# A two-layer transformer block: attention with undivided probabilities, and values by seven half-size products

## The chip, the cores and the metric

The kernel runs on one core of a Trainium2 chip. A core has a matrix engine (TensorE, PE in the profile, with its weight loads as PEld), a vector engine (VectorE, DVE), an engine for activation functions (ScalarE, ACT), a general one (GpSimd, POOL) and a queue that issues DMA transfers (SyncE, SP). Each engine works through its own instructions in the order in which they were written; semaphores hold an instruction back until what it needs is there. TensorE writes to eight banks of PSUM (2 KB in each of 128 partitions); everything else lies in SBUF or in DRAM. The metric is the time of one execution on the device in microseconds, the median of several runs.

## What is computed

The input x has 8 batches of 512 tokens with 256 channels, all in float32. The first layer adds to x a causal attention with 16 heads of 64 channels on the normalised input, and an int8 matrix product of that input. The second layer adds a gated comparison and a recurrent-style feed-forward part. Cut to the attention, which is what matters here:

```python
def _L0_attn_ref(x, Wq, bq, Wk, bk, Wv, bv, Wo, bo):
    q = (x @ Wq + bq).reshape(b, s, H, L)
    k = (x @ Wk + bk).reshape(b, s, H, L)
    v = (x @ Wv + bv).reshape(b, s, H, L)
    q = _apply_rope(q, cos, sin)
    k = _apply_rope(k, cos, sin)
    ...
    scores = jnp.einsum('bnqd,bnkd->bnqk', q, k) / jnp.sqrt(jnp.float32(L))
    scores = jnp.where(causal, scores, -1000000000.0)
    attn = jax.nn.softmax(scores, axis=-1)
    attended = jnp.einsum('bnqk,bnkd->bnqd', attn, v)
    attended = jnp.transpose(attended, (0, 2, 1, 3)).reshape(b, s, H * L)
    return attended @ Wo + bo

x = x + _L0_attn_ref(xn, ...) + _L0_ffn_ref(xn, ...)
xn = _layernorm(x, axis=-1)
x = x + _L1_attn_ref(xn, ...) + _L1_ffn_ref(xn, ...)
```

## The kernel before

The attention is worked through in 16 groups, `at` = 0 to 15: a batch `b` = at // 2 and a half `g` = at % 2 of its heads, so 8 heads a group. Everything is written in one fixed order by hand, and each engine keeps to it; there is no scheduler.

For each group the stages are these (line numbers are those of the profile of before):

- **project** (`project_qk`, matmuls at L428): queries and keys, four matmuls of 512 columns each for two half-groups. A float32 matmul appears as two instructions in the profile. ScalarE moves each bank out with its bias (L434, `l`), four DMAs on SP make a copy with neighbouring partition blocks exchanged (`y`, L436), VectorE multiplies `l` and `y` by the cosine and sine tables (L446, 128x1024 each; called rotations below), and GpSimd adds the two (L461). The tiles `l` and `y` exist twice.
- **project_v** (L472): the values of a group, for 512 tokens and 512 columns, as four banks of two matmuls (the 256 channels are contracted in two halves of 128). ScalarE copies each bank out (L478), and SP stores the result in DRAM (`va`); `load_v` loads it back in another layout (`vr`).
- **scores** (L509): 16 query blocks of 32, in five runs, 0 to 4: run 0 holds the blocks 15, 14 and 0, run 1 holds 13, 1, 12 and 2, and so on to run 4, which holds block 7. A block sees only the keys up to its own place.
- **soften**: VectorE adds the causal mask, writes the masked scores into a tile `p` and finds their maxima (L537); ScalarE takes the exponential and its sums (L541).
- **divide**: VectorE inverts the sums of a run (L552), and GpSimd multiplies each block's probabilities by them (L560; ScalarE in two places, L558).
- **turn** (L580): VectorE transposes a run's probabilities in 32x32 blocks into the tiles `t`.
- **weigh** (L597): TensorE multiplies the values by the transposed probabilities, into four banks; it needs all five runs of its group. **keep_weighed** (L611): ScalarE copies the four banks out and adds the values' bias.
- **finish**: `output_product` (L390), two banks of 128x256 products with Wo, and `add_output` (L399), which adds them to x in `x1s` on VectorE.

The main loop runs over `at` = 1 to 14 and is one pass of a pipeline over several groups. In the order of writing a pass holds: scores of run 0 of `at`; turn of run 4 of `at - 1`; soften; weigh and keep_weighed of `at - 1`; rotations of the keys of `at + 1`; divide; run 1; turn of run 0; projection of the queries of `at + 1`; run 2; rotations of their first half; turn of run 1; values of `at + 1`; run 3; rotations of the second half; turn of run 2; run 4; finish of `at - 1`; turn of run 3; projection of the keys of `at + 2`; divide. Into some passes other work is set: normalising the input of a later batch (`look_at`, `prepare`, passes 2, 3, 5, 7, 9 and 11), turning it by transposes and DMAs (`turn_x`), and the int8 product of two batches (`add_quantised`, passes 12 and 13). After pass 14, which ends behind the values, the last two groups are written out by hand together with the first steps of the second layer, and then a loop runs over the 8 batches of the second layer.

PSUM banks are handed out in turn, eight in all, each free again when its last reader has finished. TensorE's matmuls, in the order of a pass: sc (run 0), av, sc (run 1), pq, sc (run 2), pv, sc (runs 3 and 4), pw, pq.

## Time and profile before

| what | value |
|---|---|
| three runs | 935.48, 935.68, 936.91 us; median 935.68 |
| span of the profiled execution | 934.3 us |
| granted TensorE clock in it | 1.000 |
| weighings of passes 1, 7, 8 and 14 start at | 72.52, 344.75, 388.99, 658.81 us |
| last weighing (group 15) starts at | 729.87 us |

One execution was recorded by the hardware profiler; its span is the time from its first to its last instruction. The page lists busy time by engine, then a chain that is followed back from the last instruction: at each step to what released it, or to the instruction before it on the same engine. A timeline row gives start, duration, engine, line, operation, `out<-in`, shapes, the number of instructions merged into the row, and in brackets the idle time before it and what ended that. Starts of consecutive instructions on one engine can lie closer than their durations, since they overlap a little.

Over a pass in the middle of the loop, from 318.2 to 362.4 us, TensorE was busy for 44.20 of 44.20 us, VectorE for 39.40, ScalarE for 26.32 and GpSimd for 27.35.

### The profile page before, as it was taken

To read this page: it belongs to the slowest core of one execution; us is meant where nothing else is said; L and a number is where in the kernel's file an instruction comes from. 1 tells how busy PE (TensorE), PEld (TensorE's weight loads), DVE (VectorE), ACT (ScalarE), POOL (GpSimd) and SP (SyncE) were. 2 spreads that over 40 slices of the span, in tenths; PEclk is the share of its full clock that TensorE was granted. 3 is DMA by queue.
4 is the path that set the end of the run, shared out by engine and by line. 5 is a ranking of instruction groups with operands and counts; after the bars stand their busy time and mean duration, and the time that the engine had idled before them with its cause. 6 is when DMAs were issued, how large, how long until landed. Compare 5 with 4: busy or idle time off the path is not lost.

```text
span 934.3 us, 27432 instructions
## 1 busy us (share of the span) xinstructions
PE 919.8 (98%) x10451; PEld 594.7 (64%) x10451; DVE 793.3 (85%) x2441; ACT 528.3 (57%) x1478; POOL 542.2 (58%) x688
## 2 busy tenths in 40 slices
PE   9998999999999999999999999999999999999998
PEld 5446565656566575757565656566657777777776
DVE  4998898898899889988998899999899588888854
ACT  3585564647465646474746556555577444445553
POOL 2576766655665667566665756678667323444311
PEclk9999999999999999999999999999999999999999
DMA  7667354525543464245444635563435133221011
GB/s 213 194 165 213 102 138 130 121 75 132 169 105 97 109 182 132 75 115 172 123 95 114 179 93 145 151 154 97 110 108 127 47 102 79 74 50 48 25 33 34
DMA packets 70290, 108.03 MB, mean 116 GB/s; under 512 B 8592, under 2 KB 49040, under 8 KB 70160
## 3 DMA queue, kind: packets, MB, share of 16 engines
q1 hardware_dynamic: 68288, 104.64, 42.2%
q10 hardware_dynamic: 1872, 1.64, 0.7%
q8 instruction: 83, 1.36, 0.6%
q14 instruction: 47, 0.39, 0.1%
HBM read 41.76 MB, written 28.84 MB: 76 GB/s over the span
## 4 chain that ended last, share of the span: by engine, by line
PE 85%; DVE 6%; DMA 3%; issue 1%; POOL 1%; SPq 1%; ACT 1%; DVEq 0%; ACTq 0%; POOLq 0%
PE pq L428 21%; PE av L597 14%; PE sc L509 11%; PE pw L390 10%; PE pv L472 8%; PE po L756 6%; PE pk L703 3%; PE pg L718 3%; PE pvv L730 3%; DVE t L580 2%; PE c L675 2%; PE trc L743 1%; PE plr L245 1%; DVE p L537 1%; DMA xnl<-xnf 1%
## 5 line engine op out<-in xcount | busy, mean ns | idle before, releaser
L541 ACT ACTIVATE p<-p,nm 128x64 f32<-128x64 f32 (+15 forms) x512 | 260.0, 512 | 123.8 <-DVE nm L537 100.9
L560 POOL TENSOR_SCALAR p<-p,rs 128x512 f32<-128x512 f32 (+4 forms) x504 | 265.4, 547 | 44.6 <-DVE rs L552 42.6
L461 POOL TENSOR_TENSOR h<-h,y 128x1024 f32<-128x1024 f32 x62 | 161.1, 2598 | 181.5 <-DVE y L446 102.2
L537 DVE CUSTOM_DVE_ANT_0 p<-sc,cmask 128x64 f32<-128x64 f32 (+15 forms) x512 | 190.2, 434 | 53.7 <-PE sc L509 53.7
L580 DVE STREAM_TRANSPOSE t<-p 128x256 f32<-128x256 f32 (+3 forms) x640 | 192.2, 367 | 17.9 <-POOL p L560 17.8
L509 PE MATMUL sc<-h,h 64*32 64x512 f32 (+15 forms) x4096 | 138.7, 393 | 1.3 <-POOL h L461 1.2
L597 PE MATMUL av<-t,vr 32*64 32x384 f32 (+15 forms) x4096 | 128.8, 392 | 3.7 <-issue 3.7
L597 PEld LDWEIGHTS av<-t,vr 32*64 32x64 f32 x4096 | 122.8, 131 | 9.2 <-issue 7.9
L509 PEld LDWEIGHTS sc<-h,h 64*32 64x32 f32 x4096 | 78.6, 106 | 78.5 <-issue 58.3
L434 ACT ACTIVATE l<-pq,cs 128x512 f32<-128x512 f32 x128 | 84.7, 683 | 67.6 <-PE pq L428 53.3
L390 PE MATMUL pw<-wo,att 128*128 128x256 f32 x512 | 114.9, 382 | 0.8 <-DVE nm L537 0.8
L446 DVE TENSOR_TENSOR y<-y,cs 128x1024 f32<-128x1024 f32 x64 | 110.6, 1728 | 5.1 <-DMA y<-l 5.1
L428 PE MATMUL pq<-xnT,wq 128*128 128x512 f32 x256 | 114.6, 599 | 0.2 <-ACT xnT L349 0.2
L428 PE MATMUL pq<-xnT,wk 128*128 128x512 f32 x256 | 113.1, 593 | 1.4 <-DVE x L399 1.0
L472 PE MATMUL pv<-wv,xnT 128*128 128x512 f32 x256 | 114.3, 599 | 0.0
L390 PEld LDWEIGHTS pw<-wo,att 128*128 128x128 f32 x512 | 95.9, 190 | 19.5 <-issue 6.1
L541 ACT ACTIVATION_READ_ACCUMULATOR p<-p,nm 128x1 f32 x512 | 97.3, 190 | 0.0
L428 PEld LDWEIGHTS pq<-xnT,wk 128*128 128x128 f32 x256 | 48.3, 190 | 58.2 <-issue 55.4
L472 PEld LDWEIGHTS pv<-wv,xnT 128*128 128x128 f32 x256 | 47.3, 190 | 57.9 <-issue 54.5
L446 DVE TENSOR_TENSOR h<-l,cs 128x1024 f32<-128x1024 f32 x64 | 80.0, 1252 | 4.3 <-ACT l L434 4.3
L428 PEld LDWEIGHTS pq<-xnT,wq 128*128 128x128 f32 x256 | 47.2, 190 | 56.0 <-issue 48.8
L611 ACT ACTIVATE att<-av,cs 128x512 f32<-128x512 f32 x64 | 38.7, 688 | 71.3 <-PE av L597 71.3
(114 smaller groups left out, 940.7 us busy)
## 6 DMA issues: line engine op xcount, KB each, us to landing
y<-l SPq DMA_DIRECT2D x256, 128.0 KB, 2.3
va<-v SPq DMA_DIRECT2D x32, 512.0 KB, 3.1
vr<-va SPq DMA_DIRECT2D x64, 256.0 KB, 5.1
x<-in_x SPq DMA_DIRECT2D x15, 512.0 KB, 5.0
x1f<-x SPq DMA_DIRECT2D x7, 512.0 KB, 3.2
out<-y SPq DMA_DIRECT2D x14, 256.0 KB, 2.2
xnf<-xs SPq DMA_DIRECT2D x5, 512.0 KB, 3.6
xnT<-xnf SPq DMA_DIRECT2D x20, 128.0 KB, 2.8
```

The lines of the kernel that those rows point to most:

```text
L390: nc.tensor.matmul(pw[:, j, :], atts[at, p][:, tok], wo[:, 4 * (at % NH) + p, :], start=(p == 0), stop=(p == 3),)
L428: nc.tensor.matmul(pb.rearrange("p (t a r) -> p t a r", a=4, r=Q), w[:, g, k, bass.ts(t, P)], xnT[b][:, k].rearrange("p a (t r) -> p t a r ...
L434: nc.scalar.activation(l[:, t, :], pb, AF.Identity, bias=cs[:, bias : bias + 1])
L446: nc.vector.tensor_tensor(dst, src, table[:, None, :].to_broadcast([P, 2, S]), ALU.mult)
L461: (engine or nc.gpsimd).tensor_tensor(h, h, y, ALU.add)
L472: nc.tensor.matmul(pb.rearrange("p (g n) -> p g n", g=2), xnT[b][:, k, 2 * half + j], wqkv[2][:, 2 * g : 2 * g + 2, k, :], start=(k == 0), ...
L509: nc.tensor.matmul(scored[at, i][e][j * Q : j * Q + Q, :], q[rows, j % 2, bass.ts(i, Q)], k[rows, j % 2, :n], start=True, stop=True,)
L537: nc.vector.tensor_tensor_reduce(p[:, e, col : col + n], sc, cmask[:, S - n :], -1.0 / L**0.5, BIG, ALU.add, ALU.min, nm[:, c : c + 1],)
L541: nc.scalar.activation(p[:, e, col : col + n], p[:, e, col : col + n], AF.Exp, bias=nm[:, c : c + 1], scale=-1.0, accum_out=sm[:, c : c + 1],)
L560: nc.gpsimd.tensor_scalar(p, p, rs[:, c : c + 1], 1.0, ALU.mult, ALU.mult)
L580: nc.vector.transpose(turned[at][c][:, :, at_ : at_ + (n - 1) * pitch(c) + 1 : pitch(c), :], p[:, :, c * P : c * P + n * Q].rearrange("p e ...
L597: nc.tensor.matmul(banks[j][e * L : e * L + L, i * Q :], vs[at][rows, c, m, bass.ts(e, L)], t[c][rows, e, m * pitch(c) + m : m * pitch(c) ...
```

## The change

The probabilities stay undivided, so `divide` and all calls of it are gone. When the last run of a group has been turned, `settle` inverts all sums of the group at once, transposes them on VectorE, writes them to DRAM and loads them back as a tile `share`, in which each head's 64 partitions hold its reciprocal sums along the tokens. `keep_weighed` multiplies the weighted values by it, on GpSimd, and for the last group half of them on VectorE. Its bias is no longer added there: `gather_bias` multiplies Wo's rows by the values' bias and adds them up, once, and `spread_bias` sums over partitions with a matmul of ones and adds the result to the output's bias.

The values of groups 2 to 15 are computed by Strassen's scheme in Winograd's form: seven products of half the size, each two matmuls of 256 columns, in place of eight. It needs sums of the weights (`sum_weights`, once, the block `a21` overwritten), differences of the input (`mix_input`, once a batch), and additions of the products. Four of the products go to one bank `x` one after the other, with a copy after each; one goes to `y`, two to `z`.

In the loop, the output product of `at - 1`, which stood behind run 4, now stands between run 2 and run 3: its first half ahead of the seven products, its second half between them as two `fillers`. In pass 14 there are no fillers.

```diff
@@ -379,19 +378,41 @@
+        def gather_bias():
+            both = line("bvwo").rearrange("p (j n) -> p j n", j=2)
+            ones = line("ones")[:, :P]
+            nc.gpsimd.memset(ones, 1.0)
+            for p in range(NP):
+                bv = BIAS + 2 * NP + p
+                nc.gpsimd.tensor_scalar(
+                    both[:, min(p, 1), :], wo[:, p, :], cs[:, bv : bv + 1], None, ALU.mult
+                )
+                if p:
+                    nc.gpsimd.tensor_tensor(both[:, 0, :], both[:, 0, :], both[:, 1, :], ALU.add)
+            nc.gpsimd.tensor_tensor(bob, bob, rw[:, 2, :], ALU.add)
+            gathered[0] = ones, both[:, 0, :]
+
+        def spread_bias():
+            pb = bank("bvwo")
+            nc.tensor.matmul(pb[:, :D], *gathered.pop(0), start=True, stop=True)
+            nc.vector.tensor_tensor(bob, pb[:, :D], bob, ALU.add)
...
-        def output_product(at, half):
+        def output_product(at, half, js=(0, 1)):
...
@@ -481,6 +502,84 @@
+        def sum_weights():
+            one, two, three = (wv_sums[:, :, n] for n in range(3))
+            (a11, a12), (a21, a22) = ([wv[:, :, h, k] for k in range(NK)] for h in range(2))
+            for dst, x, y, op in (
+                (one, a21, a22, ALU.add), (two, one, a11, ALU.subtract),
+                (a21, a11, a21, ALU.subtract), (three, a12, two, ALU.subtract),
+            ):
+                nc.gpsimd.tensor_tensor(dst, x, y, op)
...
+        def mix_input(b):
+            t = work.tile([P, 4, 2, P], F32, tag="tx", name=f"tx_{b}")
+            (b11, b12), (b21, b22) = ([xnT[b][:, k, 2 * h : 2 * h + 2] for h in range(2)] for k in range(NK))
+            for dst, x, y in ((0, b12, b11), (1, b22, t[:, 0]), (2, b22, b12), (3, b21, t[:, 1])):
+                nc.gpsimd.tensor_tensor(t[:, dst], x, y, ALU.subtract)
+            mixes[b] = t
+
+        def project_v_by_seven(at, fillers=(None, None), between=lambda: None):
...
+            def product(to, left, right, fresh=False):
+                for j in range(2):
+                    nc.tensor.matmul(
+                        to[:, j, :], left[:, j], right, start=fresh and j == 0, stop=True,
+                        skip_group_check=j > 0 or not fresh,
+                    )
...
+            def keep(half, g_):
+                nc.scalar.copy(part(half, g_), of(x))
+
+            def add(bank_, half, g_):
+                nc.vector.tensor_tensor(part(half, g_), of(bank_), part(half, g_), ALU.add)
...
+            product(x, b11, a11, True)
+            keep(0, 0)
+            product(y, b21, a12, True)
+            product(z, t1, s1, True)
+            product(x, t2, s2)
+            keep(1, 0)
+            add(y, 0, 0)
+            if fillers[0]:
+                fillers[0]()
+            product(x, t3, s3)
+            keep(1, 1)
+            if fillers[1]:
+                fillers[1]()
+            add(z, 1, 1)
+            product(x, t4, a22)
+            keep(0, 1)
+            store(0)
+            between()
+            product(z, b22, s4)
+            add(z, 1, 0)
+            store(1)
...
@@ -544,23 +643,21 @@
-        def divide(at, run, on_act=False):
-            _, sm, rs = sums_of[at]
...
+        def settle(at):
+            sm = sums_of.pop(at)[1]
+            rs = small.tile([P, Q], F32, tag="rs16", name=f"rs_{at}", bufs=2)
+            turned_ = small.tile([P, Q], F32, tag="rt16", name=f"rt_{at}", bufs=2)
+            nc.vector.reciprocal(rs, sm)
+            nc.vector.transpose(turned_, rs)
+            there = away.tile([4, 2, S], F32, tag="rs", name=f"rsf_{at}")
+            nc.sync.dma_start(there.rearrange("j e (i q) -> (j e i) q", q=Q), turned_)
+            shares[at] = work.tile([P, 4, S], F32, tag="share", name=f"share_{at}")
+            for e in range(2):
+                nc.sync.dma_start(
+                    shares[at][e * L : e * L + L], there[:, e, :][None].to_broadcast([L, 4, S])
+                )
@@ -603,12 +700,14 @@
-                bv = BIAS + 2 * NP + 4 * g + j
-                nc.scalar.activation(atts[at, j], av, AF.Identity, bias=cs[:, bv : bv + 1])
+                if at == last and j % 2:
+                    nc.vector.tensor_tensor(atts[at, j], av, shares[at][:, j, :], ALU.mult)
+                else:
+                    nc.scalar.copy(atts[at, j], av)
+                    nc.gpsimd.tensor_tensor(atts[at, j], atts[at, j], shares[at][:, j, :], ALU.mult)
@@ -846,6 +940,7 @@
             turn(at - 1, 4)
+            settle(at - 1)
             soften(at, 0)
@@ -875,10 +969,13 @@
             project(at + 1, 0)
+            if at == 1:
+                sum_weights()
+            if g == 1:
+                mix_input(b + 1)
@@ -900,11 +996,19 @@
             if at == 1:
-                nc.gpsimd.tensor_tensor(bob, bob, rw[:, 2, :], ALU.add)
+                gather_bias()
+            elif at == 2:
+                spread_bias()
                 add_biases(0)
-            project_v(at + 1)
             if at == last - 1:
+                project_v_by_seven(at + 1)
                 break
+            output_product(at - 1, 0)
+            add_output(at - 1, 0)
+            project_v_by_seven(
+                at + 1, [lambda j=j: output_product(at - 1, 1, (j,)) for j in range(2)],
+                lambda: add_output(at - 1, 1),
+            )
@@ -912,17 +1016,14 @@
             soften(at, 3)
             turn_qk(2 * at + 3, 0)
             turn(at, 2)
-            divide(at, 3)
             scores(at, 4)
             soften(at, 4)
...
-            finish(at - 1)
             turn(at, 3)
```

The tiles of the sums change their column order to suit `settle`, and the launch asks for a DMA scratch of 1024 bytes.

## Prediction

> **What bounds the kernel now.** I read the page's busy shares first, then the chain of waits through the loop over groups, then the vector engine's timeline between two weighings. The page:

> ```profile
> PE 919.8 (98%) x10451; PEld 594.7 (64%) x10451; DVE 793.3 (85%) x2441; ACT 528.3 (57%) x1478; POOL 542.2 (58%) x688
> ```

> TensorE is never idle for long, but VectorE (DVE) is close behind it. The chain (start, duration, work) over one pass of the loop, from one value projection (pv) to the next:

> ```profile
> 319.54 7.06 PE pv L472 x16
> 326.60 2.32 PE sc L509 x80
> 328.92 7.10 PE pw L390 x32
> 336.03 6.91 PE pq L428 x16
> 342.94 1.89 PE sc L509 x45
> 344.82 7.95 PE av L597 x164
> 352.77 2.04 PE sc L509 x56
> 354.82 7.07 PE pq L428 x16
> 361.88 1.94 PE sc L509 x64
> ```

> Nothing but TensorE, 44.28 us a pass. The order matters: values (pv), scores of runs 3 and 4, output product (pw), keys' projection (pq), scores of the next group's run 0, weighing (av). Between the scores of runs 3 and 4 and the weighing that needs them lie pw, pq and one sc. What VectorE does there (its timeline: start, duration, operation):

> ```profile
> 327.83 0.45 DVE L537 CUSTOM_DVE_ANT_0 p<-sc,cmask 128x320 f32<-128x320 f32 x1
> ...
> 330.56 1.22 DVE L446 TENSOR_TENSOR h<-l,cs 128x1024 f32<-128x1024 f32 x1
> 331.69 1.22 DVE L446 TENSOR_TENSOR y<-y,cs 128x1024 f32<-128x1024 f32 x1
> 332.83 2.78 DVE L580 STREAM_TRANSPOSE t<-p 128x256 f32<-128x256 f32 x9
> 335.53 0.20 DVE L552 RECIPROCAL rs<-sm 128x4 f32<-128x4 f32 x2
> 335.65 0.39 DVE L537 CUSTOM_DVE_ANT_0 p<-sc,cmask 128x256 f32<-128x256 f32 x1
> ...
> 336.31 1.28 DVE L399 TENSOR_TENSOR x<-pw,x 128x512 f32<-128x512 f32 x2
> 337.51 2.83 DVE L580 STREAM_TRANSPOSE t<-p 128x256 f32<-128x256 f32 x10
> 340.27 0.12 DVE L552 RECIPROCAL rs<-sm 128x2 f32<-128x2 f32 x1
> 341.45 0.77 DVE L580 STREAM_TRANSPOSE t<-p 128x256 f32<-128x256 f32 x2 [1.06 <-POOL p L560]
> 344.05 0.69 DVE L537 CUSTOM_DVE_ANT_0 p<-sc,cmask 128x512 f32<-128x512 f32 x1 [1.82 <-PE sc L509]
> ```

> Masking of run 3, two rotations, transposition of run 2, masking of run 4, output added, transposition of run 3, a wait for GpSimd's division, transposition of run 4. It ends at 342.2 and TensorE weighs at 344.8: covered, with 2.6 us to spare. In the pass that also normalises an input, masking starts late (374.09) and that spare is 0.5 us (388.5 against 388.99).

> **The change, part by part.** *Values.* Eight products of 512 columns (16 instructions, 7.06 us) become 28 instructions of 256 columns. pw is the same shape: its 32 start at 373.13 and the next stage at 380.15, so 0.219 us each; 28 make 6.14 us, 0.92 less, 12.9 us over 14 groups if TensorE stays the bound. Weight loads double with the products, but pw already has one per instruction.

> *Waits inside the seven.* Four products pass through one bank, so three wait for ScalarE's copy of the one before: a copy is 0.59, with about 0.25 for two signals. In 13 groups at least 1.75 us of other products or output products lie between: nothing. In group 15 there are no fillers: two gaps of 0.85. The last product also waits for a VectorE addition (of three new ones a group, 0.65 each as L399), which is queued behind masking and transposing of runs 2 and 1 and, in some passes, normalising.

> *Division.* 504 GpSimd multiplies (265.4 us), 8 on ScalarE and 144 small reciprocals (17.1 us busy) go. Instead each group has a reciprocal and a transposition of 128x32 on VectorE (neither shape is in the trace; between 0.12 and 0.3 us together by L552 and the narrow transposes, I take 0.25, and it lies after the weighing's release), one store and two loads through DRAM on SP's queue, and four GpSimd multiplies of 128x512 (1.27 each, as the additions of x1e; two of the last group's on VectorE). The round trip: 2.3 us (as y) plus 5.1 (vr) to 8.5 (x1e), so shares land 7.9 to 11.3 us after the weighing starts; its results leave ScalarE from 8.7 (396.99 + 0.69 against 388.99). SP holds the loads back until the store has landed; behind them stand the next values' loads, which wait for the weighing's end (7.95) anyway. The multiplies are thus done by 14 to 16.5, pw starts at 19.0. Behind them on GpSimd wait the two additions of the keys (2.36 each, done by 19 to 21.5), whose y buffers the next queries' four-part DMAs on SP need; those are wanted at 22 (run 2's scores start 17.06 after the weighing, 361.81 - 344.75, and the second rotation 5 later). So zero, and about 1 us a pass if the round trip passes 11.

> *Order.* The output product moves from behind run 4 to between runs 2 and 3. Here I see the cost. The cover of the VectorE chain shrinks from 2.32+7.02+7.01+1.88 to 2.32+7.01+1.88 = 11.2 us. The chain itself, from start to start in the rows above without reciprocals, output additions and GpSimd wait: 2.73+2.27+2.70+0.66+2.76 and half of 0.77 (weighing needs the first of the last two for its start: in group 0 they ran from 69.24 to 72.74 with ten others, and av began at 72.52) = 11.51. Before it, masking starts 1.15 after its scores start (363.00 after 361.81); after it, 0.17 for the signal. 12.83 against 11.2: TensorE waits 1.6 us before every weighing. VectorE cannot start earlier, since the scores of run 3 come after all values. A pass is then 19.00 (av to pv) + 7.02 + 6.14 + 12.83 = 45.0 us against 44.3.

> *Sum.* From the first weighing of the loop (72.52) to the fourteenth (658.81) are 13 passes, 586.3 us: their 44.3 plus some 10 us of waits and extra work. After: 13 x 45.0 = 585.0. Waits for the input's DMA before pq (1.05 and 0.35 us) vanish in the 1.6. On the path remain the transposed input of batch 2 (1.2) and in two passes the quantised product's four VectorE instructions (L215, 0.474 each, 0.4 apart: 3.2 together), which now extend the chain. Then GpSimd's four new differences (128x256, 0.70 each by L380) every second pass: behind the multiplies, the keys and a power (L158, 1.02) they run about 19.8 to 22.6, while the two rotations run from 21.0. The trace shows such a meeting:

> ```profile
> 393.50 3.34 POOL L461 TENSOR_TENSOR h<-h,y 128x1024 f32<-128x1024 f32 x1 [5.80 <-DVE rs L552]
> 394.54 3.39 DVE L446 TENSOR_TENSOR y<-y,cs 128x1024 f32<-128x1024 f32 x1
> ```

> The rotation takes 3.39 instead of 1.22: it waits until GpSimd's addition is through. By this row each rotation can lose up to one difference, 0 to 1.4 a pass; I take 0.7. It counts in the five passes that normalise an input, where VectorE reaches its addition for the last product 0.1 us before TensorE wants it: 3.5 us. So 592.9, 6.6 more than now.

> [...]

> Around the loop: the first weighing comes 0.8 earlier (0.60 of GpSimd wait and 0.2 of reciprocals gone). In group 14's pass rotations precede the value additions on VectorE, so the last product waits until about 688.6, run 3's scores start at 689.5 instead of 684.9, and the next weighing comes at 703.7 instead of 701.5: +2.2, in which the 1.2 us wait for GpSimd at 691.9 is already gone. Summing weights and gathering the bias on GpSimd (some 5 and 10 us by 1.27 and 0.70) lie in passes 1 and 2 where it has 9 us and more free; spreading it is two matmul instructions and one addition, under 1 us, inside the 1.6. The smaller DMA scratch changes no instruction. Behind 703 TensorE has no gap above 0.1 us and the change adds nothing to it. Span: 934.3 + 6.6 - 0.8 + 2.2 = 942.3. The runs' median, 935.68, is 1.4 above the profiled span: **943.7 us**.

> **Rivals.** *The cover is enough (0.10).* Then TensorE stays the bound: 934.3 - 12.9 - 0.8 + 1.4 = 922 us. For it: 98% busy, and VectorE's 1.06 and 1.82 of idle time before the weighing go. Against: both are already out of the 11.51. It decides where that chain with its two ends is under 11.2, which needs 1.6 us off rows that do not vary by 0.1 between passes.

> *Break-even (0.14).* The pass costs 45.0, but the differences never meet a rotation and the quantised additions hide: 942.3 - 3.5 - 3.2 + 1.4 = 937. For: both are sized on the trace's worst place. Against: GpSimd's order puts the multiplies first.

> *Hand-overs dominate (0.08).* If ScalarE or VectorE is over a microsecond late at the value copies, each of 14 groups pays two gaps of 0.85, some 20 us more: 963. For: ScalarE's exponentials of run 2 end 5.7 us after that run's scores start, and the first copy is wanted at 6.4. Against: that is still early.

> **How the numbers follow.** The forecast has 0.68. Its own range: the pass 0.3 shorter (13 x 0.3 and no meeting: 936) to 0.4 longer with the full meeting (952). With the rivals, 932 to 953. A measurement here tells about 0.2%, 1.9 us. Faster (under 933.8): 0.10 and a little of break-even, 0.12. Same: most of break-even, 0.14. Slower: 0.74.

> **What would show it.** TensorE idle 1.5 us before most weighings, released by VectorE's transposes; its busy time some 13 us lower and the span longer; VectorE idle before the value additions and run 3's masking; passes near 45; rotations over 1.3 us in every second pass; granted clock still 1.00, as in the window around the 2.31 us gap at 70.2. I am wrong if passes are near 43.4 with weighing released by TensorE, or if idle time stands between the seven products.

## The result, and the profile after

| | before | after |
|---|---|---|
| median of 4 runs | 936.29 us (935.48 to 937.20) | 1043.62 us (1041.91 to 1046.14) |
| span of the profiled execution | 934.3 us | 1042.4 us |
| TensorE busy in it | 919.8 us | 947.1 us |
| mean granted clock | 1.000 | 0.969 |
| first to fourteenth weighing of the loop (13 passes) | 586.3 us | 685.2 us |
| from the last weighing to the end | 204.4 us | 205.4 us |

The changed kernel takes 1.1148 times as long (95% interval 1.1127 to 1.117). The forecast was 943.7 us. The loss lies in the loop over groups; behind the last weighing the two differ by 1 us. The busy line and the clock line of the page of after (the clock in tenths, 40 equal slices of the span):

```profile
PE 947.1 (91%) x10621; PEld 635.2 (61%) x10621; DVE 812.9 (78%) x2374; ACT 517.3 (50%) x1468; POOL 399.4 (38%) x294
PEclk9999998999899989999999899999997999999999
```

TensorE now idles for 1042.4 - 947.1 = 95.3 us instead of 14.5, and although the seven products take work off it, it is busy for 27.3 us more: together the 108.1 us of the two spans. The extra busy time goes with the clock, which was at half speed in 13 stretches, 64.8 us in all, before the end; TensorE was busy for 56.6 us of them, so half speed cost some 28 us. Where the idle time lies shows in TensorE's timeline of after over one pass (start, duration, work, and in brackets the idle time before it and what ended it):

```profile
288.57 8.05 PE L694 MATMUL av<-t,vr 32*64 32x512 f32 x256 [1.01 <-ACT l L455]
...
311.16 1.89 PE L538 MATMUL pv<-wv,xnT 128*128 128x256 f32 x8
316.17 3.40 PE L538 MATMUL pv<-wv_sums,tx 128*128 128x256 f32 x8 [3.12 <-POOL tx L523]
...
325.70 1.13 PE L538 MATMUL pv<-wv_sums,xnT 128*128 128x256 f32 x4 [0.94 <-DVE v L553]
326.76 2.39 PE L608 MATMUL sc<-h,h 64*32 64x320 f32 x80
329.08 7.13 PE L449 MATMUL pq<-xnT,wk 128*128 128x512 f32 x16
...
339.61 1.88 PE L694 MATMUL av<-t,vr 32*64 32x512 f32 x26 [1.52 <-ACT l L455]
```

Three stops. The last, 1.52 us before the weighing, is the one that was forecast: from the scores of run 3 (326.76) to the weighing (339.61) pass 12.85 us. The row blames ScalarE. By the timelines its last copies of queries and keys, which stand behind run 4's exponentials, ran to 339.58, and the transposes of VectorE to 339.83, of which the weighing needs all but the last: the two are level, and both go back to the masking of runs 3 and 4. The second, 0.94 us, is the last product, which waits for VectorE's addition to a half of the values. The first, 3.12 us, was not forecast: the third product waits for GpSimd's differences of the input. GpSimd's timeline tells what these differences stood behind:

```profile
303.87 4.98 POOL L710 TENSOR_TENSOR att<-att,share 128x512 f32<-128x512 f32 x4 [16.69 <-ACT l L455]
308.81 5.64 POOL L482 TENSOR_TENSOR h<-h,y 128x1024 f32<-128x1024 f32 x2
314.42 1.01 POOL L157 TENSOR_TENSOR rstd_a<-ve_a,mhalf 128x4 f32<-128x4 f32 x1
315.41 0.71 POOL L523 TENSOR_TENSOR tx<-xnT 128x256 f32<-128x256 f32 x1
```

The multiplications by the shares start at 303.87, 15.3 us after the weighing, though ScalarE had copied the weighed values out from 296.66 on, at 8.1. Over the whole execution the page's row of these multiplications says for what GpSimd had waited (busy time and mean ns of one, then idle time before them and what ended most of it):

```profile
L710 POOL TENSOR_TENSOR att<-att,share 128x512 f32<-128x512 f32 x62 | 80.2, 1326 | 270.2 <-DMA share<-rsf 204.2
```

And SP's queue in the same pass shows why the shares were late:

```profile
287.39 4.95 SPq L457 DMA_DIRECT2D y<-l  x8
292.44 0.53 SPq L655 DMA_DIRECT2D rsf<-rt  x1
295.71 1.29 SPq L658 DMA_DIRECT2D share<-rsf  x2
297.09 2.62 SPq L588 DMA_DIRECT2D vr<-va  x4
```

The sums were inverted and transposed at 289.2. Their store stands behind the eight DMAs of the keys and leaves at 292.44; it lands by 295.7; the second of the two loads lands at 303.7. In the 14 passes the multiplications start 13.3 to 18.5 us after the weighing. Everything behind them on GpSimd is late too: the keys' additions (which free the buffers that the queries' DMAs fill, and so hold back VectorE's rotations: DVE waited 57.4 us in all for the landing of `y`, 5.1 before), and the differences. One pass earlier VectorE's rows show how a late rotation reaches the values: the addition at 271.14, for which the last product waited 3.55 us, stands behind a rotation that waited 6.58 us.

```profile
265.47 1.23 DVE L467 TENSOR_TENSOR y<-y,cs 128x1024 f32<-128x1024 f32 x1 [6.58 <-DMA y<-l]
266.62 2.84 DVE L677 STREAM_TRANSPOSE t<-p 128x256 f32<-128x256 f32 x10
...
271.14 1.27 DVE L553 TENSOR_TENSOR v<-pv,v 128x512 f32<-128x512 f32 x2
```

The four largest of TensorE's waits over the whole execution (us in all, times, longest) name the same places; the kernel before has none of them:

```profile
PE pv L538 <- DVE v L553: 27.0, 13, 4.6
PE pv L538 <- POOL tx L523: 18.8, 10, 3.7
PE pw L412 <- POOL att L710: 11.2, 16, 1.5
PE av L694 <- ACT l L455: 9.5, 7, 1.5
```

The third finding is in the windows around that stop (length; busy time and instructions of PE, PEld, DVE, ACT, POOL; granted clock; share of the DMA engines; GB/s):

```profile
313.05:316.17 3.12, 0.00 (x1) 0.00 (x0) 0.63 (x1) 0.00 (x0) 3.07 (x3) 0.92 0.73 167
316.17:319.40 3.23, 3.23 (x8) 2.50 (x9) 3.23 (x9) 0.00 (x0) 3.20 (x4) 0.55 0.54 122
319.40:323.00 3.60, 3.60 (x18) 3.17 (x17) 3.57 (x8) 1.17 (x2) 2.08 (x1) 1.00 0.00 0
```

From 315.65 on, still in the stop, the clock is half for 3.4 us: two products, 8 instructions, take 3.40 us instead of the 1.89 of the two before them. So this stop of 3.12 us cost 1.51 us more behind it.

### The profile page after: what moved, and what is told of

Read it like the earlier page. It is cut to its first block, busy times and chain, and to the rows that moved or that the text cites. A ratio compares the mean times of both kernels' runs of the same rounds, so it can differ in the third digit from the quotient of the medians.

```text
span 1042.4 us, 27360 instructions
## 1 busy us (share of the span) xinstructions
PE 947.1 (91%) x10621; PEld 635.2 (61%) x10621; DVE 812.9 (78%) x2374; ACT 517.3 (50%) x1468; POOL 399.4 (38%) x294
## 3 DMA queue, kind: packets, MB, share of 16 engines
q1 hardware_dynamic: 79296, 121.68, 45.6%
## 4 chain that ended last, share of the span: by engine, by line
PE 38%; DVE 22%; DMA 15%; POOL 12%; SPq 6%; issue 4%; ACT 3%; DVEq 0%; POOLq 0%; ACTq 0%
PE av L694 8%; DVE t L677 7%; DMA vr<-va 6%; POOL att L710 5%; PE po L855 5%; POOL h L482 5%; DVE p L636 4%; SPq L457 4%; PE sc L608 4%; DVE y L467 4%; DMA y<-l 3%; PE pk L802 3%; PE pg L817 3%; PE pvv L829 3%; PE pw L412 2%
## 5 line engine op out<-in xcount | busy, mean ns | idle before, releaser
L482 POOL TENSOR_TENSOR h<-h,y 128x1024 f32<-128x1024 f32 x62 | 154.4, 2500 | 191.5 <-DVE y L467 153.8
L710 POOL TENSOR_TENSOR att<-att,share 128x512 f32<-128x512 f32 x62 | 80.2, 1326 | 270.2 <-DMA share<-rsf 204.2
L608 PE MATMUL sc<-h,h 64*32 64x512 f32 (+15 forms) x4096 | 146.1, 411 | 4.5 <-POOL h L482 2.9
L694 PE MATMUL av<-t,vr 32*64 32x448 f32 (+15 forms) x4096 | 133.2, 398 | 13.3 <-ACT l L455 9.5
L412 PE MATMUL pw<-wo,att 128*128 128x256 f32 x512 | 126.6, 393 | 14.1 <-POOL att L710 11.2
L694 PEld LDWEIGHTS av<-t,vr 32*64 32x64 f32 x4096 | 123.0, 133 | 23.5 <-ACT l L455 10.0
L467 DVE TENSOR_TENSOR y<-y,cs 128x1024 f32<-128x1024 f32 x64 | 82.3, 1286 | 68.6 <-DMA y<-l 57.4
L412 PEld LDWEIGHTS pw<-wo,att 128*128 128x128 f32 x512 | 97.0, 194 | 38.1 <-POOL att L710 18.8
L550 ACT COPY v<-pv 128x512 f32<-128x512 f32 x56 | 32.8, 586 | 136.6 <-PE pv L538 136.6
L467 DVE TENSOR_TENSOR h<-l,cs 128x1024 f32<-128x1024 f32 x64 | 91.4, 1429 | 5.2 <-ACT l L455 5.2
L449 PEld LDWEIGHTS pq<-xnT,wk 128*128 128x128 f32 x256 | 48.2, 192 | 66.8 <-issue 55.1
L709 ACT COPY att<-av 128x512 f32<-128x512 f32 x62 | 31.9, 599 | 64.0 <-PE av L694 64.0
L787 ACT ACTIVATE e<-c,nb 128x512 f32<-128x512 f32 x32 | 21.7, 683 | 74.7 <-DVE nb L782 74.2
```

Of the source, the lines that this page charges most:

```text
L412: nc.tensor.matmul(pw[:, j, :], atts[at, p][:, tok], wo[:, 4 * (at % NH) + p, :], start=(p == 0), stop=(p == 3),)
L449: nc.tensor.matmul(pb.rearrange("p (t a r) -> p t a r", a=4, r=Q), w[:, g, k, bass.ts(t, P)], xnT[b][:, k].rearrange("p a (t r) -> p t a r ...
L467: nc.vector.tensor_tensor(dst, src, table[:, None, :].to_broadcast([P, 2, S]), ALU.mult)
L482: (engine or nc.gpsimd).tensor_tensor(h, h, y, ALU.add)
L608: nc.tensor.matmul(scored[at, i][e][j * Q : j * Q + Q, :], q[rows, j % 2, bass.ts(i, Q)], k[rows, j % 2, :n], start=True, stop=True,)
L694: nc.tensor.matmul(banks[j][e * L : e * L + L, i * Q :], vs[at][rows, c, m, bass.ts(e, L)], t[c][rows, e, m * pitch(c) + m : m * pitch(c) ...
```

## The experiments

The kernel before, run beside them, had medians of 936.95 to 937.5 us. "Passes" are the 13 from the first to the fourteenth weighing: 586.3 us before, 685.2 after.

**The division's path taken away, or moved (e2, e1).** e2 is the changed kernel without `settle` and without the multiplications:

```diff
             turn(at - 1, 4)
-            settle(at - 1)
             soften(at, 0)
...
                     nc.scalar.copy(atts[at, j], av)
-                    nc.gpsimd.tensor_tensor(atts[at, j], atts[at, j], shares[at][:, j, :], ALU.mult)
```

> The changed kernel without the division: no reciprocals, no round trip through DRAM, no multiplications by the shares; the weighted values are left undivided. Queue theory: without the wait for the shares what is left is the shorter cover of the VectorE chain, 1.6 us a pass, so 936 to 948 us, and little less than the kernel with late multiplications. Seven theory: above 1010 us, since only 80 us of GpSimd time and some DMAs go that are not on the path.

It took 952.27 us (949.39 to 953.23; ratio 1.0149, 1.0122 to 1.0175), 4 us above the queue theory's range and far below the seven theory's. Passes 3 to 11 take 45.03 to 45.94 us, four of them 45.03 or 45.04 (45.0 forecast), and the weighing waits as forecast:

```profile
393.63 1.88 PE L694 MATMUL av<-t,vr 32*64 32x512 f32 x26 [1.52 <-ACT l L455]
```

So the order, the seven products, the differences and the bias cost 15 us against the kernel before run beside it (937.2), where 7.4 were forecast, and the division's path the other 91 us (1043.6 - 952.3).

e1 keeps the path but lets GpSimd do the multiplications last, behind the keys' additions, the sums and the differences:

```diff
...
             if g == 1:
                 mix_input(b + 1)
+            multiply(at - 1)
```

> The changed kernel with one thing moved: in the loop, GpSimd's four multiplications by the shares stand behind the keys' additions and the input's differences instead of ahead of them. Queue theory (the shares land about 15 us after the weighing starts, and the multiplications that wait for them hold up the keys' additions, the y buffers, the queries' rotations and the differences that the third product needs): the 3.1 us waits before the third product go, the granted clock returns to 1.00, passes fall from 51-55 to 45-46, time 940 to 955 us. Rival, seven theory (the hand-overs between the seven products and the lower clock cost the time, whatever GpSimd's order): passes stay above 50, time above 1025 us.

The queue theory missed: 1028.38 us (1025.32 to 1030.44; ratio 1.0968, 1.0941 to 1.0995). The time is in the range of the seven theory, but e2 rules that one out. The wait changed its place: the output product now waits for the multiplications 27 times, 37.6 us in all. GpSimd's and TensorE's rows in one odd pass:

```profile
404.15 6.90 POOL L704 TENSOR_TENSOR att<-att,share 128x512 f32<-128x512 f32 x4
```

```profile
406.45 2.44 PE L412 MATMUL pw<-wo,att 128*128 128x256 f32 x4 [4.45 <-POOL att L704]
```

In odd passes the multiplications now stand behind a power that waits for VectorE and four differences, and the output product, which the change had moved forward, waits for them instead. A late input that is moved back in a queue is still late for whoever needs it.

**One part of the change alone (e3, e4).** e3 is the kernel before with `finish(at - 1)` ahead of the values. e4 is the kernel before with seven products in place of eight, no fillers, and its own division and order.

```diff
+            if at < last - 1:
+                finish(at - 1)
             project_v(at + 1)
...
-            finish(at - 1)
             turn(at, 3)
```

> The kernel before with one thing moved: the output product and its addition stand between run 2 and the values instead of behind run 4; division and eight products stay. Cover theory: the VectorE chain from run 3's scores to the weighing has 11.2 us of TensorE work beside it instead of 18.2 and is, with reciprocals and the wait for GpSimd's division, about 14.1 us long: 2.9 us of wait before every weighing, 13 passes, 960 to 980 us. Rival (the order costs nothing, since VectorE was idle there before): 934 to 938 us.

```diff
...
-            project_v(at + 1)
+            project_v_by_seven(at + 1)
...
```

> The kernel before with the seven products in place of eight for groups 2 to 15, without fillers; division on GpSimd and the output product's place stay. Hand-over theory: two gaps of 0.85 us for ScalarE's copies against 0.92 us saved, so 0.8 us a group lost, 945 to 955 us, more if GpSimd's divisions delay the differences. The seven products as announced: 922 to 926 us. Seven theory (they are what costs 108 us): above 1000 us.

e3 took 1009.14 us (1008.3 to 1010.62; 1.0767, 1.0747 to 1.0788), passes of 49.5 to 51 us in the middle; e4 took 1029.78 (1028.46 to 1030.16; 1.0983, 1.0964 to 1.1003), passes of 48 to 54. Both lost more than the theories that named a cause gave, in the direction named; e4 lies in the range of its seven theory, which e2 rules out for the changed kernel. In e3 the weighing waits 3.9 us, and the granted clock behind it is 0.50 from 374.89 to 378.20:

```profile
369.02 1.96 PE L509 MATMUL sc<-h,h 64*32 64x512 f32 x48
374.89 10.71 PE L597 MATMUL av<-t,vr 32*64 32x512 f32 x256 [3.91 <-DVE t L580]
```

The weighing takes 10.71 us instead of 8.05 (the one at 72.52 in the kernel before). In e4 TensorE waits between the products 30.9 us in all for ScalarE's copies (33 times, up to 1.7 us), 23.6 for VectorE's additions (up to 3.96 before the last product) and 13.9 for GpSimd's differences. So each of the two, alone, is worse than both together without any division (e2, 952.3): there the fillers cover the hand-overs, and with the divisions out of the chain the wait before the weighing is 1.5 us instead of 3.9.

**The price of the clock (e10).** e3 with three useless matmuls of 512 columns (2.6 us) in the wait:

```diff
             banks = [bank(f"av_{at}_{j}") for j in range(4)]
+            if at < last - 2:
+                for _ in range(3):
+                    nc.tensor.matmul(banks[0], ident, cmask, start=True, stop=True)
```

> The kernel before with the output product moved (its passes took 49.8 us, with 3.86 us without matmuls before each weighing and a granted clock of 0.966), and three matmuls of 512 columns without use, 2.6 us, put into that gap in 13 passes. Clock theory (a gap of 3 us and more is followed by 3.4 us at half the clock, which cost some 1.7 us a pass): the clock stays at 1.00 and passes fall to about 48.1, 980 to 992 us, although 34 us of work are added. Rival (the clock follows the run, not the gap, or costs nothing): passes stay at 49.8 or grow, 1005 to 1015 us.

The clock theory's range holds it: 990.33 us (989.01 to 990.95), 18.8 less than e3 although 2.6 us of matmuls were added to each of 13 passes. The clock was 0.995 instead of 0.966, most middle passes 48.2 to 48.7 instead of 49.5 to 51. The same two stages:

```profile
362.31 2.84 PE L594 MATMUL av<-cmask,ident 128*128 128x512 f32 x6
366.22 8.03 PE L600 MATMUL av<-t,vr 32*64 32x512 f32 x256 [1.06 <-DVE t L580]
```

The wait is as long as it was (2.84 + 1.06 for 3.91), but the weighing is back to 8.03, with the clock at 1.00 over the two stages. 18.8 us over 13 passes are 1.45 us a pass for the throttled clock alone.

**The round trip on another queue (e7, e8, e9, e11).** In e7 store and loads go through ScalarE's DMA queue, the loads issued behind run 0's exponentials, and GpSimd multiplies between the keys' additions and the differences. e8 is e7 with only the first half of the output product as fillers and the second behind run 4. e9 is e7 with eight products and the output product behind run 4, so undivided probabilities and the bias alone. e11 is e9 with the loads behind run 1's exponentials and the multiplications behind the queries' projection.

```diff
-            settle(at - 1)
+            fetch_shares = settle(at - 1)
             soften(at, 0)
+            fetch_shares()
...
-            nc.sync.dma_start(there.rearrange("j e (i q) -> (j e i) q", q=Q), turned_)
+            queue.dma_start(there.rearrange("j e (i q) -> (j e i) q", q=Q), turned_)
...
```

> The changed kernel with the same arithmetic, but in the loop the sums' store and the shares' loads are issued from ScalarE's queue (the loads behind the exponentials of run 0), so that they no longer stand behind the keys' eight DMAs on SP, and GpSimd multiplies behind the keys' additions and ahead of the differences. Queue theory: shares land about 11 to 12 us after the weighing starts instead of 13 to 18, the multiplications are through by 17, ahead of the output product at 19, the keys' additions by 10; passes near the 45.0 of the kernel without division, 950 to 960 us. Rival, load theory (16 MB more of DMA traffic and the multiplications' use of SBUF slow everything, wherever they stand): above 1000 us.

> As the kernel with ScalarE's queue, and the output product is split: its first half fills the gaps of the seven products, its second half stands behind run 4 again. Cover theory: TensorE work beside the VectorE chain grows from 11.2 to 14.7 us against 12.8 and one addition, so no wait before the weighing; passes 43.4 to 44.5, 922 to 938 us, below the kernel before. If the wait for the last addition of the seven products decides instead (the first copy is wanted 3.5 us earlier, with VectorE still turning run 1): passes 46 to 48 and the half clock with them, 965 to 1000 us.

> As the kernel with ScalarE's queue, but with eight products as before and the output product behind run 4 as before: of the change only the undivided probabilities and the bias are left. Queue theory: TensorE is the bound as in the kernel before, passes 44.2 to 44.6, 930 to 937 us. Load theory: slower than before by more than 20 us.

> As the kernel with undivided probabilities only (eight products, output product behind run 4, shares by ScalarE's queue; 984 us, TensorE stopped for 2 to 4 us inside or just behind the weighing with no releaser, while the shares' loads kept the DMA engines fully busy). The shares' loads are moved behind the exponentials of run 1, so that they run beside the queries' projection, and the multiplications behind it. Fetch theory (in the weighing TensorE runs through some 500 short instructions, and their fetch by DMA stands behind the loads): the stops go, the granted clock is 1.00, passes 44.2 to 44.8, 930 to 938 us. Rival (undivided probabilities cost time by themselves, through GpSimd's work or the lengthened output path): above 960 us.

e7 took 989.33 us (984.13 to 1000.61; 987.71 without the longest), e8 997.97 (995.51 to 998.3), e9 984.13 (978.76 to 991.08), e11 983.6 (980.84 to 986.39). The first theory of each missed. e7's rival missed too; the second ones of e8, e9 and e11 gave a range that holds the time. For e8 the reason does not hold: the last addition of the values cost TensorE 1.8 us in all, while ScalarE's copies between the products cost 23.0 and stops with no named cause 25. With the new queue and place (e7) 54 to 56 us of the loss went. In e9 the multiplications start 11.1 to 12.5 us after the weighing but for pass 1 (18.5), in good time; yet undivided probabilities alone, with output product and values where the kernel before has them, still cost 47 us. e9 stopped TensorE with nothing named as the cause:

```profile
416.54 0.96 PE L608 MATMUL sc<-h,h 64*32 64x448 f32 x10
421.76 2.92 PE L608 MATMUL sc<-h,h 64*32 64x448 f32 x48 [4.26 <-issue]
```

"issue" means that no semaphore shows a wait, and the stop falls in the middle of a stage whose inputs are long there. During it the DMA engines were full (share 1.07, 221 GB/s). Twelve stops over 1 us with no named cause make 30.6 us of this execution. In e11 such stops were gone from passes 3 to 11 (44.6 to 45.6 us, one of 46.9). Of the 40 us that its 13 passes lost, 34 lie in passes 1 and 2 (58.1, 51.6) and in 12 and 13 (55.7, 52.5). In these last two the int8 product waited 5.8 us for VectorE, which stood in a rotation's wait of 5.2 us for the landing of `y`, with the DMA engines at a share of 0.87 in the 12 us before. So the late place, with the multiplications moved as well, took one cost away and brought another.

**The traffic alone (e13, e14).** The kernel before, with two loads of 512 KB a pass that nobody reads; beside the weighing in e13, behind run 1's exponentials in e14.

```diff
...
             soften(at, 0)
+            extra_loads(at)
...
```

> The kernel before with two loads of 512 KB a pass that nothing waits for (rows of the table repeated into 64 partitions each), issued behind the exponentials of run 0, so beside the weighing. Fetch theory: TensorE stops without a releaser for 2 to 4 us in or behind most weighings, with half the clock after it, 965 to 995 us. Rival (DMA traffic that nobody waits for is free at a mean of 116 GB/s): 935 to 940 us.

> The same extra loads, issued behind the exponentials of run 1, so beside the queries' projection, where TensorE needs 16 instructions in 7 us. Fetch theory: 935 to 945 us, with no stop above 1 us behind the weighing. Rival (the traffic itself costs, by delaying the kernel's other DMAs): as the kernel with the loads beside the weighing, or more.

e13: 979.41 us (972.91 to 981.36; 1.044, 1.04 to 1.048). e14: 960.46 (957.96 to 962.0; 1.0247, 1.0222 to 1.0273). No instruction waits for these loads, yet e13 lost 42 us, as the fetch theory had it, and nearly as much as e9 with the same traffic (47). e14 missed both its theories: the stops are gone, but 23.5 us remain. In its profile 22.9 of the 24.4 us that the 13 passes lost lie in passes 1, 2, 12 and 13, where e11 lost most too, and VectorE waits 29.7 us in all for the landing of `y` (7.5 in e13). One of e13's stops, in TensorE's timeline and in the window ahead of it (columns as above):

```profile
216.52 6.10 PE L597 MATMUL av<-t,vr 32*64 32x448 f32 x200
226.62 0.32 PE L597 MATMUL av<-t,vr 32*64 32x32 f32 x9 [4.00 <-issue]
```

```profile
218.00:222.60 4.60, 4.60 (x167) 4.38 (x153) 4.60 (x5) 0.41 (x4) 3.38 (x2) 1.00 1.03 255
```

The weighing breaks off after 200 of its matmuls. The DMA records of the trace hold packets of 16 KB on a queue of the kind "instruction" (q8); in the kernel before 74 of them are sent between 60 and 760 us, 3.4 to 21.4 us apart, 9.4 in the median. Their landing beside the end of each stop of e13 that has no named cause and is over 2 us, but for the one at 70 us, which the kernel before has as well:

```
stop of TensorE      packet sent  landed   stop ends after landing by
222.62 -> 226.62     223.81       225.17   1.45
368.33 -> 371.57     368.77       370.12   1.45
419.99 -> 422.95     420.01       421.37   1.58
511.31 -> 513.75     510.95       512.31   1.44
563.42 -> 565.64     562.66       564.08   1.56
613.03 -> 616.63     613.83       615.19   1.44
```

The nine stops without a named cause and over 1.5 us in e9 between 130 and 760 us end 1.3 to 1.7 us after such a landing too (the one above: landed 420.12, on at 421.76). The regularity is strong. That the packets carry TensorE's next instructions, and that the bulk loads held them up, is the author's reading, and it was not shown; but moving the loads away from the weighing (e14, e11) removed these stops from the middle passes, as that reading had it.

**The 91 us taken apart (e15, e17, e16).** Three variants of the changed kernel. e15 keeps store, loads and multiplications, but multiplies by the cosine table, so nothing waits for the shares. e17 keeps the multiplications by that table and has no `settle` at all. e16 keeps the wait: the same DMAs at the same places, but each load fills one partition, 8 KB, in place of 64.

```diff
...
-                    nc.gpsimd.tensor_tensor(atts[at, j], atts[at, j], shares[at][:, j, :], ALU.mult)
+                    nc.gpsimd.tensor_tensor(atts[at, j], atts[at, j], cs[:, :S], ALU.mult)
```

> The changed kernel with its reciprocals, its store and its loads of the shares, and as many multiplications, but these multiply by the cosine table instead of by the shares: nothing waits for the loads, and the division is left out. Queue theory (the wait for the shares is what costs, with what stands behind it): near the kernel without division, 950 to 965 us. Rival (the traffic and the multiplications as such): above 1000 us.

> The changed kernel with no settling at all (no reciprocals, no store, no loads), but with the multiplications of the weighted values at their place, by the cosine table; the division is left out. It has neither wait nor traffic. If the multiplications themselves lie in GpSimd's idle time, as the prediction had it: 950 to 958 us, like 952.3 without them. If four more instructions with two inputs on GpSimd are a part of the 32 us between 952.3 and 983.9: 962 to 984 us; the rest of the 32 is then traffic.

```diff
...
-                nc.sync.dma_start(
-                    shares[at][e * L : e * L + L], there[:, e, :][None].to_broadcast([L, 4, S])
-                )
+                nc.sync.dma_start(shares[at][e * L : e * L + 1], there[:, e, :][None])
```

> The changed kernel with the same store, the same two loads at the same places and the same wait of the multiplications for them, but each load fills one partition (8 KB) of a tile set to ones once, in place of 64 (512 KB); so the output is divided in two partitions of 128 alone. The wait stays, the traffic goes. If the wait for the shares in GpSimd's queue makes most of the 91 us between 1043.6 and 952.3: 1000 to 1015 us (the 60 us that lie between 1043.6 and 983.9, where nothing waited, on top of 952.3), a little less if small loads land sooner. If the traffic makes most of it, also by making the shares late: 955 to 975 us. TensorE's stops with no releaser should be gone by the fetch theory.

| | no wait for the shares | GpSimd waits for the shares |
|---|---|---|
| loads of 1 MB a pass | e15: 983.92 (978.69 to 988.24) | changed kernel: 1043.62 |
| no such traffic | e17: 957.61 (955.79 to 959.96) | e16: 970.00 (965.5 to 976.14) |

Without multiplications (e2) it is 952.3, so these cost 5.3 us, the wait alone 12.4, the traffic alone 26.3, and both together 86.0: 47.3 more than the two apart. ("The traffic alone" and "the wait alone" each hold the reciprocals, the transposition and the store of 16 KB as well, which were not tried apart.) So neither theory of a single cause holds for the whole, though e16 lies where the traffic was to be the larger one, e17 where the multiplications cost little, and e15 between its two; and four more instructions of two inputs a group on GpSimd cost these 5.3 us in all by themselves. The link between the two shows in when the multiplications start after the weighing: at 8.6 to 9.3 us in e17, 8.6 to 13.8 in e16, 13.3 to 18.5 in the changed kernel. The store's place behind the keys' DMAs and the landings of small transfers make up to 5.2 of these microseconds, the size of the loads another 4.7; the first mostly fit into GpSimd's slack, the second do not. e7 points the same way: it keeps both the traffic, from another queue, and the wait, but the keys' additions no longer stand behind the multiplications, and its time is within 6 us of e15's.

In e16 no stop without a named cause is over 0.3 us, as the fetch theory had it. But this does not tell the theories apart, since the changed kernel itself has only one over 1 us (1.65 us) and e15 one (2.79 us). So such stops, which cost e9 and e13 so much, are next to nothing of the 91 us. What the traffic costs in e15 shows elsewhere: `y` lands after 3.2 us in the median instead of 2.3 in e17, VectorE waits 33.2 us for it instead of 14.2, and TensorE waits 10.9 us for the value additions instead of 2.9.

No run was faster than the kernel before.

## Why the prediction was right and wrong

**The bound and the values: right.** With the division's path out (e2), the middle passes are 45.03 us and up to 0.9 more for 45.0, which holds 28 half-size instructions at 0.219 us each and the fillers over the hand-overs. e4 shows what the hand-overs cost where fillers and order are missing. The sign of being wrong that the prediction named, idle time between the seven products, did come, 49.9 us in all, but from the division's path: in e2 it is 3.7. So the rival of the hand-overs had seen that late value additions are dear, though not what would make them late.

**The order step: right.** "12.83 against 11.2: TensorE waits 1.6 us before every weighing." Measured 12.85 and 1.52, with ScalarE's last copies level with VectorE's chain; in e2 the wait stands before 11 of the 14 weighings of the loop, 1.25 to 2.15 us. The rival that the cover is enough is out; break-even is out as well, since even without any division the time is 952.3.

**The division step: wrong, and this is the step that failed.** It read: "So zero, and about 1 us a pass if the round trip passes 11." Three things in it were mis-sized.

First, the place in the queue. The round trip was begun at the weighing's start, with "2.3 us (as y) plus 5.1 (vr) to 8.5 (x1e)". The rows give inverted sums at +0.7, then 3.2 us behind the keys' eight issues of `y`, 3.3 for the store, and 8.2 from the issue of the loads to the first multiplication: that begins at +15.3 in place of 7.9 to 11.3. The working named what stands behind the store on SP, and not what stands ahead of it.

Second, the traffic. The loads were costed by the time to land, as if the DMA engines were free, and not as 1 MB a pass that others have to share. That alone is 26 us in e15, and as much traffic put into the kernel before costs 23 (e14) to 42 us (e13).

Third, what a late multiplication does. The sentence's own price, 1 us a pass, holds where it was meant: in e16, where the multiplications start at 8.6 to 13.8, the wait costs 12.4 us over 14 groups, 0.9 each on average (from nothing to 3.2 us by pass, comparing the profiles of e16 and e17). Past that it does not go on at this rate. In the changed kernel wait and traffic together cost 86.0 / 14 = 6.1 us a group. By the rows this is because the keys' additions, the queries' DMAs, the rotations and the differences shift together, until TensorE stops at several places a pass; e7, where the keys' additions go first, fits this.

**The clock sentence: wrong.** "granted clock still 1.00, as in the window around the 2.31 us gap at 70.2" took one gap that did no harm as a rule for all; the last section shows where that gap fell, so there was luck in it. The clock is 0.969 in after; e10 prices it at about 1.45 us for a wait of 3.9. Half clock lasted 3.4 us or a multiple of it in these runs, and about 2 us of idle time within one window of 3.413 us was enough for it (86 of 86 windows), as the last section shows.

**The smaller terms.** e2 is 8.6 us above the forecast. Gathering the bias was put at 10 of "some 5 and 10 us" of GpSimd time, in a pass with "9 us and more free"; it ran from 98.4 to 114.1 in e2, 15.7 us, and in pass 1 the scores waited 2.9 us for the keys' addition behind it. Group 14's pass took 48.1 us instead of the 44.9 forecast (703.7 - 658.8). The meeting of GpSimd's work with rotations in the passes that normalise an input, put at 0.7 us each, is at most 0.4 to 0.6 in e17 (passes 3, 5, 7 and 9 take 45.50 to 45.63 against 45.07 for passes 6 and 10, though pass 8, without such a meeting, takes 45.69), and nothing in e2, which has no multiplications ahead of the differences (45.03 or 45.04 in the same four).

**The sign** was right, and for the smaller part of the reason: order, values and bias together cost 15 us (952.3 against 937.2), the division's path 91. The range, 932 to 953, left out the times of two of the prediction's own rivals, 922 and 963, to which it gave 0.10 and 0.08.

## What to carry to other kernels

A transfer that is put on a path has three prices: its place in the queue (list what is issued ahead of it, not only what comes behind), its own time, and the bandwidth that it takes from everything else at that moment; the third was paid even where nobody waited for the data (26.3 us in e15, 42 in e13, 23.5 in e14). On an in-order engine, cost a late input by the whole line of work behind it, and look for the point at which that line reaches the bounding engine: up to there it was nearly free here (0.9 us a group in e16), past it each microsecond was paid at several places (6.1 a group in the changed kernel, with the traffic). When a step makes the matrix engine wait some two microseconds or more, add the half-speed stretch that can follow (it followed 36 of 75 gaps of 1.8 to 3.4 us here, and cost about 1.45 us a pass in e3).

## What the runs showed of the hardware

**The clock after a gap.** The traces record the granted clock, which is 1.0 or 0.5. Over the 16 profiled kernels of this case, gaps of TensorE (from 10 us into the span on) against whether a stretch at half clock began in the gap or within a microsecond behind it:

```
gap, us       gaps   followed by half clock
0.9 to 1.4      66     0
1.4 to 1.8     111     8
1.8 to 2.6      50    22
2.6 to 3.4      25    14
3.4 to 4.0      25    20
over 4.0        21    21
```

```
idle in the window, us   windows   next window at half clock
under 1.3                  4133      0
1.3 to 1.7                  114      8
1.7 to 2.0                   33     15
2.0 and more                 86     86
```

In after alone half clock followed none of 253 windows with under 1.3 us, 2 of 17 with 1.3 to 2.0, and 11 of 11 with more. So in these traces a gap was harmless or not by where it fell. The gap of 2.31 us in the profile before lay across two windows, 0.8 us in one and 1.5 in the other; one of the same length inside one window would, by this table, have been followed by half clock.

**TensorE stops under bulk loads.** In the 4 us ahead of the six stops of e13 listed above the DMA engines were at a share of 0.94 to 1.10 (192 to 274 GB/s); in the stops themselves at 0.16 to 1.08. In e9's stop at 417.50 the share was 1.07 (221 GB/s). TensorE halted for up to 4.3 us (e9) in the middle of a stage without any semaphore wait, and went on 1.3 to 1.7 us after a 16 KB packet of the kind "instruction" had landed. After has one such stop over 1 us, 1.65 us up to 817.41; the packet ahead of it landed at 816.00, 1.41 us before TensorE went on. In the kernel before, packets of the same size and kind come (83), and its only gap over 1 us with no named cause is the one of 2.31 us at 70.2, at the start of a weighing while VectorE's transposes for it still ran (69.24 to 72.74). What the packets hold, and whether they were late, was not shown: from sending to landing they took 1.27 us in the median of e13 and 1.13 in the kernel before, so if they were late, it was ahead of their sending. The same bytes in smaller pieces were not tried.
